# A graph network kernel: VectorE's order fixed around the attention scores, PSUM pools kept open, the last two tiles of a half taken together, additions on GpSimd

## The chip, the cores and the metric

The kernel runs on one core of one Trainium2 chip. The metric is the device time of one execution in microseconds. The kernel before takes 974.88 us (median of three runs, 974.85 to 976.33). Its profiled execution took 973.86 us, with a span of 972.1 us from the first to the last instruction that the profile counts.

## The reference

There are 625 nodes with 1024 features, 20000 edges sorted by destination, and 8 edge types. Two graph layers run one after the other, each with a residual and a layernorm.

```python
h = x @ W                                   # layer 0: attention
al, ar = h @ a_l, h @ a_r
e = exp(-leaky_relu(al[src] + ar[dst], 0.1))
h_prime = segment_sum(e[:, None] * h[dst], src) / (segment_sum(e, src)[:, None] + EPS)
x = layernorm(x + elu(h_prime))

u = x @ root + bias                         # layer 1: relational, gated
for r in range(8):
    mean = segment_sum(x[src] * (type == r), dst) / maximum(count, 1)
    u = u + mean @ weight[r]
z = concatenate([u, x], axis=1) @ w_gate + b_gate
x = layernorm(x + tanh(u) * z + x * (1 - z))
```

## The kernel before

The nodes lie in five tiles of 125 rows (`ST = 5`). The 1024 columns are worked on in two halves of 512, so that one product fills one PSUM bank.

**Counts.** Instead of gathering rows, the kernel builds dense counts: how many edges of each type run between each pair of nodes. One-hot matrices are made on VectorE (L808), multiplied on TensorE (L832), and copied by ScalarE into `cj` (L837), one `cj` for each tile j of destinations. Beside this TensorE computes `h` (L782), and VectorE takes the two row sums `al` and `ar` (L793). A list of due steps in the loop over `NGS` blocks says after which block row sums, spreading and counts are issued.

**Scores.** `all_types(j)` adds the eight types of `cj` in three VectorE additions, c4, c2 and c1 (L845, L847, L849). `scores_of(j)` then takes, for tile j, the sum of `ar` and `al` (L865), two operations for the edge mask and the leaky relu (L868, L869), an exponential on ScalarE (L870), a product with the counts (L871), and a row sum (L872). A small value `turn` (L874), made from the row sum of tile j and read by tile j + 1, makes the tiles go one after the other. `turn_scores(j)` transposes the scores on TensorE (L883) and ScalarE copies them to `attT` (L885). `gather_h(t, j)` multiplies them with `h` (L684). Tiles 0 to 2 (`EARLY = 3`) gather while the scores are made, tiles 3 and 4 afterwards. `sums` in the text below means L865.

**Dense products.** Each fp32 product is done in three passes with fp32r parts. `prepare(count)` splits a chunk of 128 rows of a weight into three pieces: g and e on ScalarE (L998, L999), m and the final e on VectorE (L1000, L1001). There are buffers for ten such units (`UNITS = 10`), and a half needs eight (`KC`). The nodes' rows are transposed and split likewise into h, l and d (`turned_pieces`, `pieces_of`, L1009 to L1011). `dense` takes a half: for each tile eight pairs of products into one bank (L1025, L1026), and eight into a second (L1029). In tile 0 the three are taken chunk by chunk; in the others the second bank comes after the first. Two units of the next half are prepared after tile 1 and six after the last tile.

**Order of the stages.** Scores and gathering; `attend(t)`, which makes the elu, the residual and the first layernorm of tile t (L1068 to L1078, with two small GpSimd operations for the deviation, L980 and L981); root in two halves; eight relations in two halves each, with the product by counts (`pu`, L1195); the gate's four halves wgx0, wgx1, wgu0, wgu1, during which `turn_u(t)` transposes and splits u (L1223); `mix` and the last layernorm. `ins` adds incoming counts (L1134, L1136), whose transposes (L1140) give the divisors.

**What sets the order.** Loads and stores all go through SP's queue. Within each engine the tile framework's scheduler fixes the order of instructions when the kernel is built: it takes what its own model of time calls ready first, and program order between equals. A tile pool that is closed and followed by another in the same place makes the new pool's first users wait for the last readers of the old one. Before, the PSUM pools of 6 and 2 banks are closed ahead of the first score transposes and a pool of 8 is opened.

## Time and profile before

| What | us |
|---|---|
| Median of three runs (lowest, highest) | 974.88 (974.85, 976.33) |
| Profiled execution | 973.86 |
| Its span | 972.1 |
| TensorE busy | 945.3 (97%) |
| VectorE busy | 597.2 (61%) |
| ScalarE busy | 391.4 (40%) |
| GpSimd busy | 39.5 (4%) |
| First score transposes begin | 111.51 |
| Last gathers end | 166.99 |
| First product of root begins | 167.62 |
| Gate halves begin | 844.72 |
| Last product ends | 960.4 |

The profile has one row for each instruction: start, duration, engine, line of the kernel, operation, output and input. In brackets stands how long the engine was idle before it and what ended the wait. TensorE is called PE there, its weight loads PEld, VectorE DVE, ScalarE ACT, GpSimd POOL, SyncE SP. One fp32 matmul shows as two records where the two operands are fp32. Rows that follow each other closely are merged ("x12"). A busy table gives each engine's busy time within chosen stretches, and the clock that TensorE was granted, 1.00 being full speed.

### The profile page before, as it was taken

The numbers are of one execution on the slowest core, as the hardware profiler recorded it, in microseconds if no ns is written. First come the engines' busy times: TensorE is split into PE (matmuls) and PEld (weight loads), VectorE is DVE, ScalarE is ACT, GpSimd is POOL, SyncE is SP. The second block draws the span as 40 slices with busy tenths as digits, with TensorE's granted clock in tenths as the row PEclk, the third lists the DMA queues.
The fourth block names the chain that finished last, engine by engine and source line by source line (L and its number), as shares of the span: only waits on it lengthen the run. The fifth ranks groups of instructions, "written<-read, shape, count | busy, mean of one in ns | idle before, by whom it ended". The sixth has DMA issues, their size and how long they took to land.

```text
span 972.1 us, 10853 instructions
## 1 busy us (share of the span) xinstructions
PE 945.3 (97%) x4075; PEld 730.5 (75%) x4075; DVE 597.2 (61%) x960; ACT 391.4 (40%) x714; POOL 39.5 (4%) x69
## 2 busy tenths in 40 slices
PE   7999699999999999999999999999999999999995
PEld 3555445878888888888888888888888888888874
DVE  1998978976626546356265364562653644639995
ACT  1333837244434515515434345244342551433422
POOL 3000001000000000000000000000000000002123
PEclk9999999999999999999999999999999999999998
DMA  8134862442103113021122120320320211432213
GB/s 298 44 78 102 198 197 75 141 155 87 65 22 121 45 42 108 21 80 66 55 87 63 59 87 23 99 76 11 121 66 22 87 37 50 139 112 74 87 39 112
DMA packets 61631, 83.89 MB, mean 86 GB/s; under 512 B 29323, under 2 KB 29735, under 8 KB 61572
## 3 DMA queue, kind: packets, MB, share of 16 engines
q1 hardware_dynamic: 61364, 82.93, 27.6%
q8 instruction: 34, 0.56, 0.2%
q14 instruction: 25, 0.20, 0.1%
q0 software_dynamic: 208, 0.19, 0.1%
HBM read 71.36 MB, written 11.75 MB: 86 GB/s over the span
## 4 chain that ended last, share of the span: by engine, by line
PE 92%; DVE 5%; ACT 1%; DMA 1%; SPq 0%; issue 0%; POOL 0%; POOLq 0%; DVEq 0%; ACTq 0%
PE pu L1195 19%; PE p_w L1026 15%; PE p_w L1025 15%; PE p_w L1029 15%; PE ph L782 7%; PE phh L684 3%; PE p_root L1029 2%; PE p_root L1025 2%; PE p_wgx L1029 2%; PE p_wgx L1026 2%; PE p_wgx L1025 2%; PE p_root L1026 2%; PE pc L832 2%; PE p_wgu L1029 1%; PE p_wgu L1026 1%; PE p_wgu L1025 1%
## 5 line engine op out<-in xcount | busy, mean ns | idle before, releaser
L1026 PE MATMUL p_w<-m_w,x_l 128*128 128x512 f32 x640 | 249.1, 389 | 0.0
L1025 PE MATMUL p_w<-g_w,x_h 128*128 128x512 f32 x640 | 249.0, 389 | 0.0
L1195 PE MATMUL pu<-y,cf 125*128 125x512 f32 x800 | 184.4, 389 | 0.0
L1177 DVE SCALAR_TENSOR_TENSOR v<-p_w,v 125x512 f32<-125x512 f32 x80 | 55.2, 690 | 201.7 <-PE p_w L1029 153.0
L1029 PE MATMUL p_w<-e_w,x_d 128*128 128x512 f32 x640 | 176.4, 389 | 0.0
L1195 PEld LDWEIGHTS pu<-y,cf 125*128 125x128 f32 x800 | 150.2, 188 | 31.6
L1029 PEld LDWEIGHTS p_w<-e_w,x_d 128*128 128x128 f32 x640 | 120.1, 188 | 25.5 <-DVE e_w L1001 0.3
L1025 PEld LDWEIGHTS p_w<-g_w,x_h 128*128 128x128 f32 x640 | 120.2, 188 | 25.1
L1026 PEld LDWEIGHTS p_w<-m_w,x_l 128*128 128x128 f32 x640 | 120.1, 188 | 25.1 <-DVE m_w L1000 0.2
L1176 ACT ACTIVATE v<-p_w 125x512 f32<-125x512 f32 x80 | 47.6, 595 | 214.0 <-PE p_w L1026 214.0
L1000 DVE SCALAR_TENSOR_TENSOR m_w<-raw_w,e_w 128x512 fp32r<-128x512 f32 x128 | 84.9, 684 | 36.3 <-ACT e_w L999 36.3
L1180 DVE TENSOR_TENSOR y<-v,y 125x512 fp32r<-125x512 f32 x80 | 55.3, 691 | 50.8 <-ACT y L1179 50.8
L998 ACT ACTIVATE g_w<-raw_w 128x512 fp32r<-128x512 f32 x128 | 73.2, 621 | 29.8 <-PE p_w L1025 20.7
L1001 DVE TENSOR_TENSOR e_w<-g_w,m_w 128x512 fp32r<-128x512 f32 x128 | 84.9, 684 | 0.5
L1179 ACT CAST y<-v 125x512 fp32r<-125x512 f32 x80 | 49.2, 615 | 75.1 <-DVE v L1177 75.1
L782 PE MATMUL ph<-w,xT 128*125 128x512 f32 x160 | 77.6, 612 | 0.3 <-ACT xT L714 0.3
L999 ACT ACTIVATE e_w<-raw_w 128x512 fp32r<-128x512 f32 x128 | 73.2, 623 | 0.0
L1199 DVE SCALAR_TENSOR_TENSOR L_gnn_bias_dram_u<-pu,inv,L_gnn_bias_dram_u 125x512 f32<-125x512 f32 x80 | 55.5, 743 | 0.5
L1161 ACT CAST cf<-cs 128x640 fp32r<-128x640 f16 x40 | 25.9, 724 | 54.8 <-PE pu L1195 46.2
L1242 POOL TENSOR_TENSOR L_gnn_bias_dram_u<-L_gnn_bias_dram_u,xr 125x512 f32<-125x512 f32 x10 | 17.4, 1743 | 744.2 <-ACT L_gnn_bias_dram_u L1227 712.0
L684 PE MATMUL phh<-h_sb,attT 125*125 125x512 f32 x100 | 45.9, 614 | 0.4 <-ACT attT L885 0.4
L782 PEld LDWEIGHTS ph<-w,xT 128*125 128x125 f32 x160 | 27.9, 192 | 24.1 <-issue 22.2
(159 smaller groups left out, 972.0 us busy)
## 6 DMA issues: line engine op xcount, KB each, us to landing
raw_w<-in_L_gnn_weight_dram SPq DMA_DIRECT2D x64, 512.0 KB
cd<-cj SPq DMA_DIRECT2D x40, 160.0 KB
cs<-cd SPq DMA_DIRECT2D x8, 800.0 KB
x<-in_x_dram SPq DMA_DIRECT2D x8, 512.0 KB
w<-in_L_gnn_W_dram SPq DMA_DIRECT2D x8, 512.0 KB
raw_root<-in_L_gnn_root_dram SPq DMA_DIRECT2D x8, 512.0 KB
raw_wgx<-in_L_gnn_w_gate_dram SPq DMA_DIRECT2D x8, 512.0 KB
raw_wgu<-in_L_gnn_w_gate_dram SPq DMA_DIRECT2D x8, 512.0 KB
```

What stands on the lines that cost most here:

```text
L684: nc.tensor.matmul(banks_h[t, half][:n, :], attT[:nj, j, tile_cols(t)], h_sb[:nj, j, half * HALF:(half + 1) * HALF], start=(j == 0), stop= ...
L782: nc.tensor.matmul(p[:n, :], xT[:, k, :n], w0_sb[k][:, half * HALF:(half + 1) * HALF], start=k == 0, stop=k == KC - 1)
L998: nc.scalar.activation(g, w, AF.Copy, scale=DOWN)
L999: nc.scalar.activation(e, w, AF.Copy, scale=UP12 * DOWN)
L1000: nc.vector.scalar_tensor_tensor(m, w, UP12, e.bitcast(F32), op0=OP.mult, op1=OP.subtract)
L1001: nc.vector.tensor_tensor(e, g.bitcast(F32), m.bitcast(F32), op=OP.subtract)
L1025: nc.tensor.matmul(p1, h[:, k, :], g, start=k == 0, stop=False, skip_group_check=True)
L1026: nc.tensor.matmul(p1, l[:, k, :], m, start=False, stop=k == KC - 1, skip_group_check=True)
L1029: nc.tensor.matmul(p2, d[:, k, :], e, start=k == 0, stop=k == KC - 1, skip_group_check=True)
L1180: nc.vector.tensor_tensor(lo[:n], v[:n], hi[:n].bitcast(F32), op=OP.subtract)
L1195: nc.tensor.matmul(p, c[:m, t, j * 128:(j + 1) * 128], piece[:m], start=(t == 0 and i == 0), stop=(t == ST - 1 and i == 1), skip_group_che ...
L1199: nc.vector.scalar_tensor_tensor(at, p[:n], inv[:n, j, r:r + 1], at, op0=OP.mult, op1=OP.add)
```

## The change

1. **VectorE's order.** `in_turn` ties an instruction behind the one that was written before it on its engine. It is an edge for the order of issue only, without a wait of its own. The chain runs from the first sum of the scores to root's pieces: sum and two operations of tile 0, the first operation of tile 1, the product of tile 0, the second operation of tile 1; then in each step j the row sum of j, c4 of tile j + 3 (for j below 2), the product of j + 1, c2 and c1 of tile j + 3, and the two operations of j + 2. The value `turn` goes. The first scores' two copies to `attT` move from ScalarE to VectorE and stand in the chain. `prepare(KC, pinned=True)` puts the m of root's eight units behind all of it.
2. **GpSimd.** The sums of tiles 1 to 4 (L865), one addition of each half of the normalizing for tiles 1 to 4 (L1073), and the four additions of `ins` (L1134, L1136) move from VectorE to GpSimd.
3. **PSUM.** The pools of 6 and 2 banks stay open to the end. Until the gathering each bank names its pool; later ones are dealt out in turn, six from the first pool and two from the second.
4. **Two tiles together.** With `goes_on`, `dense` takes tiles 3 and 4 chunk by chunk side by side, all three products for both tiles. This holds for root0, root1, wgx0, wgx1 and wgu0. `turn_u` of tiles 3 and 4 moves from wgx1 into wgu0, behind its tiles 0 and 1.

```diff
-    begin = ExitStack()
-    ps = [begin.enter_context(tc.tile_pool(name="f_ps0", bufs=6, space=bass.MemoryType.PSUM))]
-    ps_h = begin.enter_context(tc.tile_pool(name="f_ps_h", bufs=2, space=bass.MemoryType.PSUM))
-
-    def bank(name):
-        return ps[0].tile([128, 512], F32, tag="bank", name=name)
+
+    ps = [ctx.enter_context(tc.tile_pool(name=f"f_ps{n}", bufs=n, space=bass.MemoryType.PSUM)) for n in (6, 2)]
+    turns = []
+
+    def bank(name, pool=None):
+
+        if pool is None:
+            pool = len(turns) % 8 // 6
+            turns.append(name)
+        return ps[pool].tile([128, 512], F32, tag="bank", name=name)
+
+    def in_turn(ins):
+
+        tc.keep_in_program_order(ins)
 
...
         for half in range(2):
             if j == 0:
-                banks_h[t, half] = bank(f"phh_{t}_{half}")
+                banks_h[t, half] = bank(f"phh_{t}_{half}", 1 if t == EARLY else 0)
...
             n = rows_of(t)
-            halves_h = [ps_h.tile([128, 512], F32, tag="ph", name=f"ph_{t}_{half}") for half in range(2)]
+            halves_h = [bank(f"ph_{t}_{half}", 1) for half in range(2)]
...
-        def all_types(j, cj):
+        def all_types(j, part, put=lambda ins: None):
 
             n = rows_of(j)
-            c4 = attp.tile([128, ST, 4, 128], F16, name="c4")
-            c4 = c4[:, :, :, :n]
-            nc.vector.tensor_tensor(c4, cj[:, :, 0:4, :n], cj[:, :, 4:8, :n], op=OP.add)
+            if part == 0:
+                c4 = attp.tile([128, ST, 4, 128], F16, name="c4")[:, :, :, :n]
+                fours.append(c4)
+                put(nc.vector.tensor_tensor(c4, cjs[j][:, :, 0:4, :n], cjs[j][:, :, 4:8, :n], op=OP.add))
+                return
+            c4 = fours.pop()
             c2 = c4[:, :, 0:2, :]
-            nc.vector.tensor_tensor(c2, c2, c4[:, :, 2:4, :], op=OP.add)
-            c1 = attp.tile([128, ST, 128], F16, name=f"c1_{j}")
-            nc.vector.tensor_tensor(c1[:, :, :n], c2[:, :, 0, :], c2[:, :, 1, :], op=OP.add)
-            ct.append(c1[:, :, :n])
+            c1 = attp.tile([128, ST, 128], F16, name=f"c1_{j}")[:, :, :n]
+            ct.append(c1)
+            put(nc.vector.tensor_tensor(c2, c2, c4[:, :, 2:4, :], op=OP.add))
+            put(nc.vector.tensor_tensor(c1, c2[:, :, 0, :], c2[:, :, 1, :], op=OP.add))
...
-
-        turn = attp.tile([128, ST], F32, name="turn")
-        nc.vector.memset(turn[:, :1], 1.0)
-
-        def scores_of(j):
+        def sums_of(j, eng):
 
             n = rows_of(j)
-            cols = slice(j * 128, j * 128 + n)
-            c1 = ct[j]
-            e = attp.tile([128, ST, 128], F32, name=f"e_{j}")
-            e = e[:, :, :n]
-            nc.vector.tensor_tensor(e, ar_b[:, cols].unsqueeze(1).to_broadcast([128, ST, n]),
-                                    al.unsqueeze(2).to_broadcast([128, ST, n]), op=OP.add)
-
-            nc.vector.scalar_tensor_tensor(e, c1, turn[:, j:j + 1], e, op0=OP.min, op1=OP.mult)
-            nc.vector.scalar_tensor_tensor(e, e, SLOPE, e, op0=OP.mult, op1=OP.max)
-            nc.scalar.activation(e, e, AF.Exp, scale=-1.0)
-            nc.vector.tensor_tensor(e, e, c1, op=OP.mult)
-            nc.vector.tensor_reduce(rsum[:, :, j], e, axis=AX.X, op=OP.add)
-            if j + 1 < ST:
-                nc.vector.tensor_scalar(turn[:, j + 1:j + 2], rsum[:, 0, j:j + 1], 0.0, 1.0, op0=OP.min, op1=OP.add)
-            return e
+            e = attp.tile([128, ST, 128], F32, name=f"e_{j}")[:, :, :n]
+            i = eng.tensor_tensor(e, ar_b[:, j * 128:j * 128 + n].unsqueeze(1).to_broadcast([128, ST, n]),
+                                  al.unsqueeze(2).to_broadcast([128, ST, n]), op=OP.add)
+            es.append(e)
+            return i
+
+        def scores_of(j, parts=(0, 1)):
+
+            if 0 in parts:
+
+                in_turn(nc.vector.scalar_tensor_tensor(es[j], ct[j], 1.0, es[j], op0=OP.min, op1=OP.mult))
+            if 1 in parts:
+                in_turn(nc.vector.scalar_tensor_tensor(es[j], es[j], SLOPE, es[j], op0=OP.mult, op1=OP.max))
+                nc.scalar.activation(es[j], es[j], AF.Exp, scale=-1.0)
+
+        def times_edges(j):
+            in_turn(nc.vector.tensor_tensor(es[j], es[j], ct[j], op=OP.mult))
+
+        def sum_scores(j):
+            in_turn(nc.vector.tensor_reduce(rsum[:, :, j], es[j], axis=AX.X, op=OP.add))
 
         def turn_scores(j, e):
             n = rows_of(j)
             for t0, t1 in ((0, 3), (3, ST)):
-                p = bank(f"patt_{j}_{t0}")
+                p = bank(f"patt_{j}_{t0}", 1)
                 for t in range(t0, t1):
                     m = rows_of(t)
                     nc.tensor.transpose(p[:n, (t - t0) * TN:(t - t0) * TN + m], e[:m, t, :], ident[:m, :m])
                 c0, c1 = t0 * TN, t1 * TN
-                nc.scalar.copy(attT[:n, j, c0:c1], p[:n, :c1 - c0])
+                if j:
+                    nc.scalar.copy(attT[:n, j, c0:c1], p[:n, :c1 - c0])
+                else:
+                    in_turn(nc.vector.tensor_copy(attT[:n, j, c0:c1], p[:n, :c1 - c0]))
...
         def counted(j):
-            all_types(j, cjs[j])
+            if j < ST - 2:
+                all_types(j, 0)
+                all_types(j, 1)
             store_counts(j, cjs[j])
+
+        def first_scores(_):
+            spread_ar()
+            in_turn(sums_of(0, nc.vector))
+            for j in range(1, ST):
+                sums_of(j, nc.gpsimd)
+            scores_of(0)
+            scores_of(1, parts=(0,))
+            times_edges(0)
+            scores_of(1, parts=(1,))
...
                     if steps == n_steps:
-                        due.append((i + 6, lambda _: spread_ar(), None))
-                        due.extend((max(i + 6 + 4 * j, (j + 1) * NG + LAG), lambda _: es.append(scores_of(len(es))), None)
-                                   for j in range(AHEAD))
+                        due.append((i + 6, first_scores, None))
...
-        begin.close()
-        ps[0] = ctx.enter_context(tc.tile_pool(name="f_ps", bufs=8, space=bass.MemoryType.PSUM))
         for _ in range(4):
             fetch()
         turn_scores(0, es[0])
         for j in range(ST):
             gather_h(0, j)
-            if len(es) < ST:
-                es.append(scores_of(len(es)))
+
+            sum_scores(j)
             if j + 1 < ST:
+                later_types = j + 3 if j < 2 else None
+                if later_types:
+                    all_types(later_types, 0, in_turn)
+                times_edges(j + 1)
+                if later_types:
+                    all_types(later_types, 1, in_turn)
+                if j + 2 < ST:
+                    scores_of(j + 2)
                 turn_scores(j + 1, es[j + 1])
             for t in range(1, EARLY):
                 gather_h(t, j)
...
-    def prepare(count):
...
-            nc.vector.scalar_tensor_tensor(m, w, UP12, e.bitcast(F32), op0=OP.mult, op1=OP.subtract)
+            rest = nc.vector.scalar_tensor_tensor(m, w, UP12, e.bitcast(F32), op0=OP.mult, op1=OP.subtract)
+            if pinned:
+                in_turn(rest)
             nc.vector.tensor_tensor(e, g.bitcast(F32), m.bitcast(F32), op=OP.subtract)
             ready.append((g, m, e))
             if i == 1:
...
+    def dense_tiles(ts, chunks, name, by_chunk):
+
+        sums = {t: (bank(f"p1_{name}_{t}"), bank(f"p2_{name}_{t}")) for t in ts}
+
+        def first(t, k, g, m):
+            h, l, _ = x1[t]
+            nc.tensor.matmul(sums[t][0], h[:, k, :], g, start=k == 0, stop=False, skip_group_check=True)
+            nc.tensor.matmul(sums[t][0], l[:, k, :], m, start=False, stop=k == KC - 1, skip_group_check=True)
+
+        def second(t, k, e):
+            nc.tensor.matmul(sums[t][1], x1[t][2][:, k, :], e, start=k == 0, stop=k == KC - 1, skip_group_check=True)
 
         for k, (g, m, e) in enumerate(chunks):
-            first(k, g, m)
-            if t == 0:
-                second(k, e)
-        if t:
+            for t in ts:
+                first(t, k, g, m)
+                if by_chunk:
+                    second(t, k, e)
+        if not by_chunk:
             for k, (g, m, e) in enumerate(chunks):
-                second(k, e)
-        return p1, p2
-
-    def dense(name, put, after=None):
+                for t in ts:
+                    second(t, k, e)
+        return sums
+
+    def dense(name, put, after=None, goes_on=False):
 
         chunks = [ready.pop(0) for _ in range(KC)]
-        for t in range(ST):
-            n = rows_of(t)
-            p1, p2 = dense_tile(t, chunks, f"{name}_{t}")
-            put(t, p1[:n, :], p2[:n, :])
-            if t == 1:
-                prepare(UNITS - KC)
-            if after:
-                after(t)
+
+
+        steps = [(t,) for t in range(ST - 2)] + ([(ST - 2, ST - 1)] if goes_on else [(ST - 2,), (ST - 1,)])
+        for ts in steps:
+            for t, (p1, p2) in dense_tiles(ts, chunks, name, ts[0] == 0 or len(ts) > 1).items():
+                n = rows_of(t)
+                put(t, p1[:n, :], p2[:n, :])
+                if t == 1:
+                    prepare(UNITS - KC)
+                if after:
+                    after(t)
         prepare(2 * KC - UNITS)
...
-            nc.vector.tensor_add(v, q[:n], v)
+            (nc.gpsimd if t else nc.vector).tensor_tensor(v, q[:n], v, op=OP.add)
...
-    prepare(KC)
+    prepare(KC, pinned=True)
...
-    dense("root0", add_to(u, 0), after=later_x1)
+    dense("root0", add_to(u, 0), after=later_x1, goes_on=True)
...
-    nc.vector.tensor_tensor(ins, ins16[:, 0, :], ins16[:, 1, :], op=OP.add)
+    nc.gpsimd.tensor_tensor(ins, ins16[:, 0, :], ins16[:, 1, :], op=OP.add)
     for t in range(2, ST):
-        nc.vector.tensor_tensor(ins, ins16[:, t, :], ins, op=OP.add)
+        nc.gpsimd.tensor_tensor(ins, ins16[:, t, :], ins, op=OP.add)
...
-    dense("root1", add_to(u, 1))
+    dense("root1", add_to(u, 1), goes_on=True)
...
-    dense("wgx0", add_to(z, 0))
-    dense("wgx1", add_to(z, 1), after=turn_u)
-    dense("wgu0", mix(0))
+    dense("wgx0", add_to(z, 0), goes_on=True)
+    dense("wgx1", add_to(z, 1), after=lambda t: t < ST - 2 and turn_u(t), goes_on=True)
+    dense("wgu0", mix(0), after=lambda t: t < 2 and turn_u(t + ST - 2), goes_on=True)
```

More of the change, by code (lines that the diff above doesn't have):

```diff
@@ L455 @@
 LAG = 4
-AHEAD = 1
 EARLY = 3
@@ L665, in load_x, with transposed @@
         return xt
-    def transposed(src_t, n, name, put):
+    def transposed(src_t, n, name, put, pool=None):
         for g in range(2):
-            p = bank(f"{name}_{g}")
+            p = bank(f"{name}_{g}", pool)
             for j in range(4):
@@ L713, in x_turned @@
             xT = xin.tile([128, KC, 128], F32, tag="xT", name=f"xT_{t}")
-            transposed(xt, n, f"px_{t}", lambda ks, p: nc.scalar.copy(xT[:, ks, :n], p))
+            transposed(xt, n, f"px_{t}", lambda ks, p: nc.scalar.copy(xT[:, ks, :n], p), 0)
             if t + 2 < ST:
@@ L735, in gather_edges @@
         def gather_edges():
-            p = bank("p_count")
+            p = bank("p_count", 0)
             for m in range(per // BLOCK):
@@ L752, in place_edges @@
         def place_edges():
-            pe = bank("p_edges")[:, :4 * NGS]
+            pe = bank("p_edges", 0)[:, :4 * NGS]
             for b in range(2):
@@ L768, in place_edges @@
                                            op0=OP.mult, op1=OP.add)
-        ct = []
+        ct, fours = [], []
         s_hots = [hot.tile([128, 2, BG, 2, 128], F16, name=f"s_hot_{i}", bufs=1) for i in range(HOTS)]
@@ L828, in counts_of @@
             s_hot, m_hot, _ = built[i]
-            p = bank(f"pc_{i}")
+            p = bank(f"pc_{i}", 0)
             at = 0
@@ L916, in spread_ar @@
             for t0, t1 in ((0, 3), (3, ST)):
-                p = bank(f"p_ar_{t0}")
+                p = bank(f"p_ar_{t0}", 0)
                 for t in range(t0, t1):
@@ L988, in fast, with prepare @@
     xp = ctx.enter_context(tc.tile_pool(name="f_x1", bufs=1, side="right"))
-    def prepare(count):
+    def prepare(count, pinned=False):
         for _ in range(count):
@@ L1017, in turned_pieces @@
         transposed(src_t, 128, f"p{name}_{t}", lambda ks, p: pieces_of(h, l, d, ks, p))
-    def dense_tile(t, chunks, name):
-        h, l, d = x1[t]
-        p1, p2 = bank(f"p1_{name}"), bank(f"p2_{name}")
-        def first(k, g, m):
-            nc.tensor.matmul(p1, h[:, k, :], g, start=k == 0, stop=False, skip_group_check=True)
-            nc.tensor.matmul(p1, l[:, k, :], m, start=False, stop=k == KC - 1, skip_group_check=True)
-        def second(k, e):
-            nc.tensor.matmul(p2, d[:, k, :], e, start=k == 0, stop=k == KC - 1, skip_group_check=True)
-        for k, (g, m, e) in enumerate(chunks):
-            first(k, g, m)
-            if t == 0:
-                second(k, e)
-        if t:
+    def dense_tiles(ts, chunks, name, by_chunk):
[6 more added lines that the diff above has]
+            nc.tensor.matmul(sums[t][1], x1[t][2][:, k, :], e, start=k == 0, stop=k == KC - 1, skip_group_check=True)
+        for k, (g, m, e) in enumerate(chunks):
+            for t in ts:
[3 more added lines that the diff above has]
+        if not by_chunk:
```

## The prediction

> **What bounds the kernel now.** I read the page's engine shares first, then the busy table by stage, TensorE's own timeline where the table shows it idle, VectorE's timeline over the same stretch, and last the places where GpSimd and VectorE meet.
>
> ```profile
> PE 945.3 (97%) x4075; PEld 730.5 (75%) x4075; DVE 597.2 (61%) x960; ACT 391.4 (40%) x714; POOL 39.5 (4%) x69
> ```
>
> TensorE sets the time: it is idle for 27 us of 972.1. The table finds these in three places: 6 us at the start and 11.6 us behind the last matmul, which the change leaves alone, and the scores, from 109 to 140 us:
>
> ```profile
> 109.00:112.00 3.00, 0.49 (x5) 0.52 (x5) 3.00 (x5) 2.94 (x7) 0.00 (x0) 1.00 0.98 201
> 114.70:119.50 4.80, 0.00 (x0) 0.00 (x0) 4.80 (x9) 4.77 (x10) 0.86 (x1) 0.82 0.73 150
> 119.50:122.00 2.50, 2.44 (x7) 1.88 (x8) 2.50 (x7) 1.71 (x4) 0.09 (x1) 0.50 0.90 235
> 122.00:124.00 2.00, 2.00 (x3) 0.67 (x2) 2.00 (x4) 0.63 (x1) 0.00 (x0) 0.50 0.78 222
> 124.00:126.00 2.00, 2.00 (x5) 0.90 (x4) 2.00 (x4) 1.78 (x4) 0.00 (x0) 0.85 0.73 269
> ```
>
> The columns are TensorE, its weight loads, VectorE, ScalarE, GpSimd, the granted clock and DMA. VectorE is full while TensorE stands still, and behind the long stop the clock is granted at half (0.50). TensorE's timeline there:
>
> ```profile
> 104.09 4.92 PE L832 MATMUL pc<-m_hot,s_hot 128*128 128x240 f16 x42
> 111.51 0.78 PE L883 MATMUL patt<-ident,e 125*125 125x125 f32 x5 [2.50 <-DVE e L871]
> 112.69 1.98 PE L684 MATMUL phh<-h_sb,attT 125*125 125x512 f32 x4 [0.40 <-ACT attT L885]
> 119.56 1.41 PE L883 MATMUL patt<-ident,e 125*125 125x125 f32 x5 [4.89 <-DVE e L871]
> 120.76 7.22 PE L684 MATMUL phh<-h_sb,attT 125*125 125x512 f32 x12
> 128.36 5.32 PE L684 MATMUL phh<-h_sb,attT 125*125 125x512 f32 x12
> ```
>
> The idle times are 2.50 + 0.40 + 4.89 and 0.21 later, 8.0 us; the half clock costs 0.5 x 4.44 + 0.15 x 2.0 = 2.5 us (7.22 against 5.32 for the same twelve records). **10.5 us** are there to be had. The clock's mean of 0.82 over 4.8 us says that it fell some 3.1 us into the stop; the 2.50 did not bring it down. What kept the second scores:
>
> ```profile
> 111.28 1.47 DVE L845 TENSOR_TENSOR c<-cj 128x2500 f16<-128x2500 f16 x1
> 117.49 1.29 DVE L1000 SCALAR_TENSOR_TENSOR m_root<-raw_root,e_root 128x512 fp32r<-128x512 f32 x2
> 118.70 0.81 DVE L871 TENSOR_TENSOR e<-e,c 128x625 f32<-128x625 f32 x1
> ```
>
> The edge sums of tile 4, two sums of later scores and root's pieces stand between the first scores (done 111.36) and the second (119.51): 8.15 us.
>
> **The change, part by part.** *VectorE's order.* It takes c4 of tiles 3 and 4 (1.38), four sums (0.72 each) and m_root out of the way. ar_b is there at 105.0. Without any contention e_0 is: sum 0.72, two operations 0.78 + 0.73, exponential 0.73 and hand-over, product 0.72: 108.9. TensorE has counts until 109.01, so the first gap would be nothing; keeping the PSUM pools open, which lets the transposes go before ScalarE's last copy (110.65), is worth something only if e_0 is early. But the order fixed also puts the second scores' first operation, which needs GpSimd's sum e_1, ahead of e_0's product: product, copies and all that follow queue behind that wait.
>
> *Sums on GpSimd.* Its addition of 512 columns takes 1.29 us undisturbed; 625 columns are an estimated 1.58. And it disturbs VectorE:
>
> ```profile
> 892.72 1.29 POOL L1242 TENSOR_TENSOR L_gnn_bias_dram_u<-L_gnn_bias_dram_u,xr 125x512 f32<-125x512 f32 x1 [5.04 <-ACT L_gnn_bias_dram_u L1227]
> 892.87 2.29 DVE L1011 SCALAR_TENSOR_TENSOR u_d<-u_l,u_h 128x512 fp32r<-128x512 f32 x2
> ```
>
> Two such operations take 1.29 elsewhere, so 1.00 is lost here. Over the ten GpSimd additions of the trace VectorE's neighbours lose 0 to 1.0, 0.56 in the mean. The Trainium skill speaks against this edit, in "SBUF — State Buffer", section "Who interferes with whom": a VectorE instruction with two SBUF inputs and a GpSimd instruction that reads SBUF use the same port, and whichever starts second is blocked until the other has finished. All of e_0's operations have two SBUF inputs. By the rule, taking turns, four additions stand in the chain: 105.0 + 3.75 + 4 x 1.58 = 115.1. By the rows: 105.0 + 2.23, e_1's addition 1.58, 0.78, 0.72 and one block of 0.56 are 110.9. I take 110.9, since back-to-back VectorE work kept GpSimd waiting in the trace (one addition took 2.70 with no loss to VectorE). First gap: 1.9, with ends 0 and 6.1.
>
> *The first copies on VectorE.* By the PSUM rows (512 columns 0.68), 375 columns cost an estimated 0.5, then 0.35; the gap behind the transposes stays 0.5.
>
> *The second scores.* Behind the product: 0.73, copies 0.95 with their wait, row sum 0.72, c4 1.38, product 0.72, and two blocks of 0.56: 116.5. TensorE, after transposes (0.78), copy (0.5) and all six gathers of step 0 (5.32), is there at 117.5: no gap. If the second transposes again stand behind two gathers only, it is there at 114.0: gap 2.5. I take 1.2. From then each step costs TensorE 0.71 + 5.32 = 6.03 and VectorE at most 5.5, so no gap grows. No stop reaches 3.1 us, so no half clock. Idle 1.9 + 0.5 + 1.2 = 3.6; the stage gains 10.5 - 3.6 = **6.9**, ends 1.4 (first gap 6.1, then 0.5, and the clock's 2.5 paid again) and 10.0.
>
> *Root's pieces behind the scores.* VectorE ends the scores at 116.5 + 13.3 = 129.8 and the reciprocals at 130.4; 16 operations of 0.60 end at 140.0. The cover is the 5.5 us in which it waits before its first normalizing operation (146.61, which comes 6.9 earlier, 139.7): cost nothing now, but that cover is used up. The five loads of weights (SP, 118.8 to 138.1) wait for these pieces and shift by some 8 us; the loads of x stand among them in SP's queue and are wanted at 139.7, the second half of root at 192: hidden.
>
> *Additions in the normalizing.* Eight of 0.68 leave VectorE (5.4); by the rows 8 x 0.56 = 4.5 come back, by the rule 8 x 1.3 = 10.4. GpSimd's rstd operations (0.55 + 0.57) queue behind the next tile's additions; x of tiles 1 to 3 is ready 7 us ahead of its transposes, so this is covered. The four additions of ins on GpSimd (an estimated 1.6 each for 3.2 on VectorE) delay the p_ins transposes in root1, 0 to 3 us. Together I take 0.5.
>
> *Two tiles together.* Units come free during the last two tiles, not in the last pass. The first two tiles of a half need 2 x 5.44 = 10.88; they take 11.26 (transposes off), 11.24 and 12.60 in the three gate halves, and up to 0.5 extra in root1: 2.5 to 3.0 lost. The longest stop:
>
> ```profile
> 942.12 2.11 PE L1029 MATMUL p_wgu<-e_wgu,u_d 128*128 128x512 f32 x8 [0.61 <-DVE e_wgu L1001]
> ```
>
> The table's row for the stretch before it:
>
> ```profile
> 898.00:929.00 31.00, 31.00 (x142) 25.31 (x141) 30.05 (x46) 14.35 (x28) 5.60 (x4) 1.00 0.24 76
> ```
>
> VectorE is busy 30.05 of these 31 us, and the change takes nothing off it there. Turning u's tiles 3 and 4 (8 transposes of 0.87 in all, four VectorE operations of 0.64, two tanh each) moves behind wgu0's tiles 0 and 1, where mixing already takes five operations of 0.69 per tile of 5.44: 3.4 + 2.6 is more than a tile, so these pieces come late by 1 to 2 us, with one tile of 5.44 in between as cover. Earlier units therefore help only partly: I take 1.0, ends -1.0 (no cover: the pair waits for u's pieces) and 2.5 (nothing lost any more). In root0 the pair brings tile 4's pieces forward:
>
> ```profile
> 185.86 1.03 PE L673 MATMUL px<-ident,x 128*128 128x128 f32 x8
> 187.13 1.29 DVE L1010 TENSOR_TENSOR x_l<-px,x_h 128x512 fp32r<-128x512 f32 x2
> 188.34 1.29 DVE L1011 SCALAR_TENSOR_TENSOR x_d<-x_l,x_h 128x512 fp32r<-128x512 f32 x2
> ```
>
> Before, d was wanted at 195.8; now 0.7 us into the pair, 187.3 on this scale, and its first half is there at 188.9: a wait of 1.6, or nothing if TensorE's queue has tile 3 in front. I take 0.7.
>
> **Sum:** 6.9 + 1.0 - 0.5 - 0.7 = 6.7. The span of 972.1 becomes 965.4; with the 1.8 around it (973.86 - 972.1) the profiled run becomes 967.2. The runs' median stands 1.0 above the profiled one: 974.88 - 6.7 = **968.2**.
>
> **Rivals.** *Likeliest, 0.56:* as summed; its own range is 964.5 to 971.5 (first gap 0.5 to 3.5, second 0 to 2.5).
> *All gaps close, 0.09:* VectorE's chain runs ahead of GpSimd and the gathers cover the second scores: 10.0 + 1.0 - 0.5, about 964 to 963. For it: GpSimd's 2.70; against it: the queue behind e_1.
> *GpSimd in turns, 0.18:* the four sums take turns with e_0's chain. The stage gains 1.4, the halves pay the pair: 973 to 976, mostly no change. For it: 1.00 lost on single additions.
> *Slower, 0.17:* VectorE becomes the bound at root0's pair. If each of the eight additions blocks it by b, it is 8b - 5.4 late and TensorE waits 1.6 + 8b - 5.4 at the pair. This outweighs 6.9 + 1.0 - 0.5 when b is above 1.4. At 1.6 the wait is 9.0, the half clock adds 2.5, and the time is 974.88 + 1.6 + 2.5 = 979. For it: VectorE is busy 38.9 of the 43.4 us from 146.6 to 190; against it: no row shows b above 1.0.
>
> **Chances.** About 0.2% (2 us) is what a measurement of this kernel can tell from no change. Faster: 0.56 + 0.09 + a third of GpSimd in turns = 0.71; same: 0.11, most of the rest of it; slower: 0.18. The range, leaving out little above and below, is 963.5 to 977.
>
> **What would show it.** The transposes of e_0 start near 111.0, those of e_1 near 117; no row at clock 0.50 after 112; the last transposes end near 136 with all earlier gathers done; m_root begins at 130. GpSimd's sums show 1.6 to 2.1, VectorE's products beside them up to 1.0 more than 0.80. In the pair, a wait on x_d. In the last half no stop on e_wgu. Wrong makes it a stop over 3 us before the first transposes, a pair wait over 3 us, or p_ins late.

## The result and the profile after

The changed kernel takes **979.25 us** (median of five runs, 978.52 to 980.88), against 975.29 for the kernel before in the same comparison: a ratio of 1.0043 with an interval of 1.0028 to 1.0058. It is slower by 0.43%, where 0.7% faster was forecast, and it lies outside the range given. The profiled execution took 978.52 us, with a span of 976.7.

From the page of the changed kernel:

```profile
PE 947.7 (97%) x4075; PEld 734.0 (75%) x4075; DVE 604.0 (62%) x941; ACT 393.5 (40%) x712; POOL 61.4 (6%) x85
```

VectorE gave sixteen additions away (with the five small instructions of `turn` gone and two copies come in, 960 instructions became 941), and yet its busy time rose from 597.2 to 604.0. What is left on it got longer. The stages, by the starts of their first products and the end of the last (960.55 before, 964.15 after):

| Stage | before, us | after, us | difference |
|---|---|---|---|
| up to root's first product | 167.6 | 163.2 | -4.4 |
| root, two halves | 59.4 | 70.1 | +10.6 |
| relations, eight times two halves | 617.7 | 617.4 | -0.3 |
| gate, four halves | 115.8 | 113.5 | -2.3 |
| behind the last product | 11.6 | 12.6 | +1.0 |

These add up to the +4.6 between the spans. The scores and the gate gained; root lost more than both. The view of what TensorE waited for, in the changed kernel (us in total, times, longest):

```profile
PE patt L894 <- DVE e L883: 3.6, 1, 3.6
PE p_root L1058 <- DVE x_l L1042: 3.1, 1, 3.1
PE p_all L1183 <- DVE in_r L1181: 2.5, 1, 2.5
```

Before, the two long waits were 4.9 and 2.5, both at `patt`. Now there are three, all on VectorE, two of them in root, where there was none. The busy table of the changed kernel around them (columns as in the prediction):

```profile
109.00:112.60 3.60, 0.03 (x1) 0.00 (x0) 3.60 (x4) 2.55 (x5) 2.96 (x2) 1.00 0.80 164
114.00:116.00 2.00, 2.00 (x3) 0.94 (x4) 2.00 (x3) 2.00 (x6) 0.00 (x0) 0.60 0.00 0
116.00:118.00 2.00, 2.00 (x4) 0.75 (x3) 1.97 (x4) 2.00 (x5) 0.00 (x0) 0.54 1.01 210
...
170.00:173.10 3.10, 0.00 (x1) 0.00 (x0) 2.11 (x5) 0.55 (x2) 1.33 (x3) 0.89 0.88 285
173.10:175.00 1.90, 1.86 (x4) 1.49 (x5) 1.90 (x4) 0.00 (x0) 0.73 (x1) 0.50 1.00 351
...
177.00:179.00 2.00, 2.00 (x6) 1.52 (x6) 1.56 (x4) 0.00 (x0) 0.79 (x2) 0.50 0.90 235
...
200.00:202.50 2.50, 0.05 (x1) 0.00 (x0) 2.50 (x5) 0.58 (x2) 0.00 (x0) 1.00 0.87 318
204.00:206.00 2.00, 2.00 (x6) 1.52 (x6) 2.00 (x4) 0.00 (x0) 0.00 (x0) 0.50 0.52 174
```

In this trace each stop is followed by some microseconds at half clock, which cost half their length: about 1.7 us behind the first, 2.9 behind the second, 1.7 behind the third. TensorE's timeline behind the first stop:

```profile
112.68 0.81 PE L894 MATMUL patt<-ident,e 125*125 125x125 f32 x5 [3.65 <-DVE e L883]
114.00 5.37 PE L691 MATMUL phh<-h_sb,attT 125*125 125x512 f32 x8 [0.51 <-DVE attT L899]
119.21 0.71 PE L894 MATMUL patt<-ident,e 125*125 125x125 f32 x5
```

The second scores no longer make TensorE wait (119.21 has no bracket). The first do, and the reason is beside them, in the timeline of VectorE and GpSimd:

```profile
104.79 0.81 DVE L868 TENSOR_TENSOR e<-ar_b,al 128x625 f32<-128x625 f32 x1 [0.89 <-ACT ar_b L935]
105.64 1.72 DVE L877 SCALAR_TENSOR_TENSOR e<-c,e 128x625 f32<-128x625 f16 x1
107.39 1.72 DVE L879 SCALAR_TENSOR_TENSOR e<-e 128x625 f32<-128x625 f32 x1
109.04 1.83 DVE L877 SCALAR_TENSOR_TENSOR e<-c,e 128x625 f32<-128x625 f16 x1
110.79 1.83 DVE L883 TENSOR_TENSOR e<-e,c 128x625 f32<-128x625 f32 x1
...
104.84 7.12 POOL L868 TENSOR_TENSOR e<-ar_b,al 128x625 f32<-128x625 f32 x4 [5.53 <-ACT ar_b L935]
```

Four additions on GpSimd, 1.78 each, and exactly four operations of VectorE that take 1.72 to 1.83 where they take 0.81 alone: each pays 0.9 to 1.0. (The second row at L877 is the first operation of tile 1, which the fixed order puts ahead of e_0's product.) The same in the normalizing and ahead of root1:

```profile
164.41 1.28 POOL L1109 TENSOR_TENSOR x<-q,x 125x512 f32<-125x512 f32 x1
164.48 1.76 DVE L1114 TENSOR_SCALAR x<-x,mv,rstd 125x1024 f32<-125x1024 f32 x1 [0.77 <-POOL rstd L1011]
167.37 1.40 DVE L1030 SCALAR_TENSOR_TENSOR m_root<-raw_root,e_root 128x512 fp32r<-128x512 f32 x1
172.40 1.28 DVE L1042 TENSOR_TENSOR x_l<-px,x_h 128x512 fp32r<-128x512 f32 x2
173.14 0.79 PE L1058 MATMUL p_root<-m_root,x_l 128*128 128x512 f32 x1 [3.13 <-DVE x_l L1042]
...
192.16 2.94 DVE L1030 SCALAR_TENSOR_TENSOR m_root<-raw_root,e_root 128x512 fp32r<-128x512 f32 x2 [0.72 <-ACT e_root L1029]
192.79 5.41 POOL L1172 TENSOR_TENSOR ins<-ins,ins 8x640 f32<-8x640 f16 x3
195.01 3.74 DVE L1033 TENSOR_TENSOR e_root<-g_root,m_root 128x512 fp32r<-128x512 f32 x2
...
201.69 0.80 DVE L1181 TENSOR_REDUCE in_r<-ins 8x1 f32<-8x640 f32 x1
202.54 0.18 PE L1183 MATMUL p_all<-ones,in_r 8*1 8x1 f32 x2 [2.49 <-DVE in_r L1181]
```

The scaling of x takes 1.76 where it takes 0.81, and two pairs of pieces take 2.94 and 3.74 where such a pair takes 1.29. At 167.37 there is something else: a piece of root1's first units, which before was done by 138.7, stands in the middle of the normalizing, ahead of tile 1's x_l (172.40). And in_r, which p_all waits for, starts at 201.69, although GpSimd is done with ins at 198.20: root1's pieces stand before it.

### The profile page after: what moved, and what is told of

It is laid out like the page before. It is cut to its first block, busy times and chain, and to the rows that moved or that the text cites. A ratio compares the mean times of both kernels' runs of the same rounds, so it can differ in the third digit from the quotient of the medians.

```text
span 976.7 us, 10888 instructions
## 1 busy us (share of the span) xinstructions
PE 947.7 (97%) x4075; PEld 734.0 (75%) x4075; DVE 604.0 (62%) x941; ACT 393.5 (40%) x712; POOL 61.4 (6%) x85
## 4 chain that ended last, share of the span: by engine, by line
PE 89%; DVE 6%; ACT 1%; issue 1%; POOL 1%; DMA 1%; SPq 0%; POOLq 0%; DVEq 0%; ACTq 0%
PE pu L1231 19%; PE p_w L1057 15%; PE p_w L1058 15%; PE p_w L1061 15%; PE ph L789 7%; PE phh L691 2%; PE p_wgx L1057 2%; PE p_wgx L1058 2%; PE p_wgx L1061 2%; PE p_root L1057 2%; PE pc L839 2%; PE p_root L1058 2%; PE p_root L1061 1%; PE p_wgu L1057 1%; PE p_wgu L1058 1%; PE p_wgu L1061 1%
## 5 line engine op out<-in xcount | busy, mean ns | idle before, releaser
L1278 POOL TENSOR_TENSOR L_gnn_bias_dram_u<-L_gnn_bias_dram_u,xr 125x512 f32<-125x512 f32 x10 | 14.0, 1405 | 739.0 <-ACT L_gnn_bias_dram_u L1263 718.5
```

## The experiments

**First theory:** the additions on GpSimd take VectorE's turns, and that is the loss. **Rival:** the fixed order of VectorE, or the two tiles together, makes the stops. Four kernels undo the GpSimd part, group by group and whole.

*The sums of the scores back on VectorE.*

```diff
-            for j in range(1, ST):
-                sums_of(j, nc.gpsimd)
             scores_of(0)
+            in_turn(sums_of(1, nc.vector))
...
+                    in_turn(sums_of(j + 2, nc.vector))
                     scores_of(j + 2)
```

> After the change, with the four sums of the scores (e_1 to e_4) back on VectorE, each just ahead of the scores that use it; all else as after. Theory (additions on GpSimd take VectorE's turns): the four VectorE operations of 1.72 to 1.83 us beside the sums fall back to about 0.80, e_0 is ready near 109.5 instead of 112.6, the stop of 3.65 us ahead of the first transposes of scores shrinks below 1 and the half clock from 114 to 118 (about 1.8 us) goes: 4 to 5.5 us faster than the changed kernel, 973.5 to 975. Rival (the fixed order of VectorE, not GpSimd, sets the first stop): the stop stays above 3 us and the time is within 1 us of the changed kernel, 978 to 980.

Measured: 975.62 us, ratio to the kernel before 1.0004 (0.9995 to 1.0012), so 3.6 us under the changed kernel. Its timeline:

```profile
107.01 0.81 DVE L877 SCALAR_TENSOR_TENSOR e<-c,e 128x625 f32<-128x625 f16 x1
111.01 0.81 PE L894 MATMUL patt<-ident,e 125*125 125x125 f32 x5 [0.61 <-DVE e L883]
...
200.15 0.18 PE L1183 MATMUL p_all<-ones,in_r 8*1 8x1 f32 x2 [2.48 <-DVE in_r L1181]
```

The operations are back at 0.81, the stop is 0.61 and its half clock is gone. That the additions lengthen these operations and make the first stop is shown; the gain is a little below what was expected. A stop of 2.2 at tile 1 and the one of 2.5 at p_all stay.

*The normalizing additions back on VectorE.*

```diff
-            (nc.gpsimd if t else nc.vector).tensor_tensor(v, q[:n], v, op=OP.add)
+            nc.vector.tensor_tensor(v, q[:n], v, op=OP.add)
```

> After the change, with the normalizing additions of tiles 1 to 4 back on VectorE; all else as after. Theory (turns): the eight beside-operations lose about 0.7 us each and x_l of tile 1 is ready 3 us or more earlier, so the stop of 3.13 us at root0's tile 1 and its half clock (about 2.8 us) go: 4.5 to 6.5 us faster, 972.5 to 974.5. Rival (units 9 and 10 of root's pieces, which now land inside the normalizing, make x_l late): the stop only shrinks by about 1 us, the half clock stays: 0 to 2 us faster, 977 to 979.

Measured: 977.70 us, 1.0026 (1.0016 to 1.0035), only 1.6 us under the changed kernel. The stop of 3.1 at tile 1 is gone with its half clock, more than the rival allowed, though the held pieces are still there. But TensorE then stands 2.1 us ahead of tile 4's transposes, 0.9 at tile 4's x_l and 3.3 ahead of root1. The rival's number was right, its reason was not: relief on VectorE at one place comes back as stops at the next.

*The additions of ins back on VectorE.*

```diff
-    nc.gpsimd.tensor_tensor(ins, ins16[:, 0, :], ins16[:, 1, :], op=OP.add)
+    nc.vector.tensor_tensor(ins, ins16[:, 0, :], ins16[:, 1, :], op=OP.add)
     for t in range(2, ST):
-        nc.gpsimd.tensor_tensor(ins, ins16[:, t, :], ins, op=OP.add)
+        nc.vector.tensor_tensor(ins, ins16[:, t, :], ins, op=OP.add)
```

> After the change, with the four additions of the in-degrees back on VectorE; all else as after. Theory (turns): the operations of VectorE beside them fall from 2.94 and 3.74 us a pair to 1.29, the stop of 2.49 us ahead of root1 and its half clock to 206 (about 1.8 us) go: 3.5 to 4.5 us faster, 974.5 to 975.5. Rival (the two tiles taken together leave no cover at root0's end, so in_r is late whoever adds): the stop stays at 2 us or more, at most 1 us faster, 978 to 979.

Measured: 976.92 us, 1.0020 (1.0011 to 1.0028): 2.3 us, less than expected. The stop of 2.5 at p_all goes; one of 0.8 at p_ins and one of 0.3 behind it are left.

*All three groups back on VectorE* (the three diffs together).

> After the change, with all three groups of additions back on VectorE, so that only the fixed order, the open PSUM pools and the two tiles together remain. Theory (GpSimd's additions are the whole loss): the three gains add up to 12 to 15 us, 964 to 967, faster than the kernel before by 0.8 to 1.1%. Rival (the fixed order delays root's stage by itself): a stop of over 2 us stays at root0's tile 1 and the time is 970 to 975.

Measured: 972.09 us, 0.9972 (0.9960 to 0.9983). GpSimd's part costs **7.2 us** in the changed kernel, close to the sum of the three (7.5). But 964 to 967 was expected. Root0 begins at 159.0 here, 8.6 us earlier than before, and still root takes 66.5 us for the 59.4 of before: stops of 1.2, 0.8 and 1.4 between 177 and 182, and half clock behind them. The first theory explains most of the loss, not all of it.

**Second theory:** from the scores to root0's last tile VectorE is the bound, and what TensorE gains in the scores only lets it run into VectorE. **Rival:** the two tiles taken together ask too early.

*Without GpSimd's additions, root1's first two units after root0's tile 3.*

```diff
-                if t == 1:
+                if t == (ST - 2 if name == "root0" else 1):
                     prepare(UNITS - KC)
```

> The kernel without GpSimd's additions (972.1), with the pieces of root1's first two units made after root0's tile 3 instead of after its tile 1; all else as there. Theory (VectorE's own queue from the end of the scores to tile 4's x sets root0's end): four operations of 0.60 us, 2.4 us, leave that queue, x of tile 4 is scaled near 178.7 instead of 181.1, the stops of 1.2, 0.8 and 1.4 us at tile 3 shrink to about 1 in sum and the half clock behind them (1.6 us) goes: 968 to 969.8. Rival (the two tiles taken together ask for tile 4's pieces too early, whatever VectorE's load): the stops stay and the time is 971 to 973.

Measured: 970.38 us, 0.9951 (0.9935 to 0.9968). x of tile 4 is scaled at 178.67, as worked out, instead of 181.07; but the units then go ahead of tile 4's x_l, which makes a stop of 2.1 behind one of 1.6. The time is between the two expectations and, with 1.7 us under the kernel that it varies, not outside what the two intervals leave.

*Without GpSimd's additions, root0's tiles 3 and 4 one after the other.*

```diff
-    dense("root0", add_to(u, 0), after=later_x1, goes_on=True)
+    dense("root0", add_to(u, 0), after=later_x1)
```

> The kernel without GpSimd's additions (972.1), with root0's last two tiles taken one after the other again; the other halves still take them together. Theory (VectorE's queue): tile 4's transposes stand ahead of most of tile 3's matrix multiplications in either form and wait for the same x at 181: 971 to 973. Rival (the two tiles together are what asks too early): the three stops of root0 and its half clock go, 3.5 to 5 us: 967 to 968.6.

Measured: 975.13 us, 1.0000 (0.9990 to 1.0009): neither; it is 3.0 us worse than with the pair. Its timeline and a row of its busy table:

```profile
181.57 0.81 DVE L1114 TENSOR_SCALAR x<-x,mv,rstd 125x1024 f32<-125x1024 f32 x1 [0.45 <-POOL rstd L1011]
182.44 1.97 PE L680 MATMUL px<-ident,x 128*128 128x128 f32 x8 [2.39 <-DVE x L1114]
...
182.40:188.00 5.60, 5.56 (x18) 4.75 (x19) 4.37 (x7) 1.19 (x2) 0.00 (x0) 0.51 0.33 101
```

TensorE waits for tile 4's x as the theory said, and works 5.6 us at half clock. So the pair does not make this stop. What makes it 3.0 us slower is in good part the clock: in the two traces TensorE's stops in root add up to 4.4 us here and 4.0 with the pair, while the half clock costs about 4.2 and 1.7. Here a second stretch of it follows, from 204 to 208, behind a stop of 0.8 ahead of root1; with the pair a stop of 0.7 there has none. The rest was not traced.

*The kernel before, with the two tiles together and the moved turns of u alone.*

```diff
-    dense("root0", add_to(u, 0), after=later_x1)
+    dense("root0", add_to(u, 0), after=later_x1, goes_on=True)
...
-    dense("root1", add_to(u, 1))
+    dense("root1", add_to(u, 1), goes_on=True)
...
-    dense("wgx0", add_to(z, 0))
-    dense("wgx1", add_to(z, 1), after=turn_u)
-    dense("wgu0", mix(0))
+    dense("wgx0", add_to(z, 0), goes_on=True)
+    dense("wgx1", add_to(z, 1), after=lambda t: t < ST - 2 and turn_u(t), goes_on=True)
+    dense("wgu0", mix(0), after=lambda t: t < 2 and turn_u(t + ST - 2), goes_on=True)
```

> The kernel before with the last two tiles of a half taken together, and the two turns of u moved, alone. Theory: the gate stage gains 2.3 us as in the changed kernel, and root0's pair waits 1 to 2 us for tile 4's pieces, which were ready at 188.4 where the pair would start at 186.7: 973 to 974.8. Rival (the pair in root0 costs several us by itself): 975.5 or more.

Measured: 983.69 us, 1.0089 (1.0072 to 1.0106). The expectation was wrong by 9 us, and in the direction of the rival. The wait for tile 4's pieces is hardly there. In its place (timeline, then busy table):

```profile
196.44 0.80 DVE L1138 TENSOR_TENSOR ins<-ins 8x640 f32<-8x640 f16 x1
204.05 0.81 DVE L1140 TENSOR_TENSOR ins<-ins,ins 8x640 f32<-8x640 f16 x1
204.95 0.34 PE L1144 MATMUL p_ins<-ident,ins 8*125 8x8 f32 x1 [6.26 <-issue]
205.46 0.80 DVE L1149 TENSOR_REDUCE in_r<-ins 8x1 f32<-8x640 f32 x1
...
198.50:205.00 6.50, 0.24 (x2) 0.08 (x1) 6.50 (x11) 0.92 (x2) 0.00 (x0) 0.69 0.27 81
205.00:210.00 5.00, 4.36 (x12) 2.54 (x12) 2.31 (x8) 0.00 (x0) 0.00 (x0) 0.50 0.77 263
```

The profile puts the wait down to no instruction ("issue"), but p_ins begins 0.09 us behind the last addition of ins (204.86). The first addition and in_r in the kernel before:

```profile
191.20 0.80 DVE L1134 TENSOR_TENSOR ins<-ins 8x640 f32<-8x640 f16 x1
...
195.06 0.81 DVE L1145 TENSOR_REDUCE in_r<-ins 8x1 f32<-8x640 f32 x1
```

With tiles 3 and 4 singly, VectorE adds tile 3's sums to u, does the additions of ins while TensorE works on tile 4, and turns to root1's pieces last. With the pair, no sums come before the pair ends; root1's pieces fill VectorE's queue first and ins comes behind and between them: its first addition starts 5 us later, in_r 10 us later. TensorE's queue has p_ins and p_all ahead of root1, so it stands 6.3 us and then works at half clock until 214.5. The order is read from the rows; why the scheduler chose it was not looked into.

*Without GpSimd's additions, root's pieces not held behind the scores.*

```diff
-    prepare(KC, pinned=True)
+    prepare(KC)
```

> The kernel without GpSimd's additions (972.1), with root's pieces no longer held behind the scores in VectorE's order, as before the change. Theory (VectorE's work up to tile 4's x is the same in any order, and it has no idle time to give): the pieces go between the scores again, root0 starts 3 to 5 us later and loses its stops: 970 to 973.5. Rival (holding the pieces behind the scores is what makes x late): the scores keep their gain and root0 its pace, 966.5 to 968.5.

Measured: 970.77 us, 0.9961 (0.9945 to 0.9977), as the theory had it; the 1.3 us under the kernel with held pieces are within the intervals. Root0 begins at 162.0, three us later (one of them because the scores themselves begin later in this trace); one stop of 0.4 is left in it, and 0.8 at p_ins behind it.

**What is left to tell apart:** which parts are good, and whether the root0 pair's harm is the order of ins.

*The order of the scores and the open PSUM pools alone:* the kernel just shown, with all halves singly and `turn_u` back in wgx1.

```diff
-    dense("root0", add_to(u, 0), after=later_x1, goes_on=True)
+    dense("root0", add_to(u, 0), after=later_x1)
...
-    dense("root1", add_to(u, 1), goes_on=True)
+    dense("root1", add_to(u, 1))
...
-    dense("wgx0", add_to(z, 0), goes_on=True)
-    dense("wgx1", add_to(z, 1), after=lambda t: t < ST - 2 and turn_u(t), goes_on=True)
-    dense("wgu0", mix(0), after=lambda t: t < 2 and turn_u(t + ST - 2), goes_on=True)
+    dense("wgx0", add_to(z, 0))
+    dense("wgx1", add_to(z, 1), after=turn_u)
+    dense("wgu0", mix(0))
```

> The kernel before with the change's order of the scores and the open PSUM pools alone: no additions on GpSimd, root's pieces not held behind the scores, no two tiles together. Theory (VectorE's queue up to tile 4's x caps what the scores give): root0 starts near 162 instead of 167.6, about 2 of the 5.6 us come back as stops in root0, and the gate keeps its own pace: 970.5 to 972.5. Rival (the score stage's gain passes whole): 968 to 970.

Measured: **968.50 us**, 0.9931 (0.9913 to 0.9949). The rival holds: root0 begins at 162.3 and takes no stop, root lasts 59.4 us, and the score stage's gain passes whole. The second theory, that VectorE caps what the scores can give, was too strong. The order, the open pools, the end of `turn` and the copies on VectorE were not tried one by one, so the gain belongs to them together.

*The kernel before with pairs in every half but root0's* (the diff of the pairs alone, without its first two lines).

> The kernel before with the last two tiles together in every half but root0's. Theory (in root0 the pair lets root1's pieces go ahead of the in-degrees' additions in VectorE's order, and TensorE then stands 6 us and runs 4 us at half clock): all of that goes and the gate's 2.3 us stay, 972 to 973.5, that is 10 to 12 us less than with root0's pair. Rival (the loss of the pairs alone comes from any of the pairs, by their PSUM banks): 978 to 984.

Measured: 973.66 us, 0.9985 (0.9978 to 0.9992), 10 us under the kernel with root0's pair, as expected, though 0.2 above the range. In its trace the gate takes 113.5 us, for 115.8 before, and root 59.4, for 70.2 with root0's pair.

*Order of the scores, and pairs in every half but root0's.*

```diff
-    dense("root0", add_to(u, 0), after=later_x1, goes_on=True)
+    dense("root0", add_to(u, 0), after=later_x1)
```

> The kernel of the run without GpSimd's additions and with unheld pieces (970.8), with root0's last two tiles one after the other. Theory: the additions of the in-degrees go ahead of root1's pieces again, so the stop of 0.8 us at p_ins and the half clock of 1.7 us from 202 to 206 go: 968 to 970. Rival (as with the held pieces, taking root0's tiles singly costs 3 us): 973 to 974.5.

Measured: **966.67 us**, 0.9908 (0.9892 to 0.9925), below the expected range, and the fastest of all: 0.9% faster than the kernel before. Busy table and timeline, with the table's rows of the kernel before behind them:

```profile
104.00:140.00 36.00, 33.27 (x142) 18.19 (x140) 34.97 (x55) 25.07 (x53) 0.95 (x1) 1.00 0.73 204
140.00:160.00 20.00, 20.00 (x54) 9.10 (x53) 18.43 (x34) 15.38 (x26) 2.16 (x4) 1.00 0.32 106
...
177.89 0.81 DVE L1114 TENSOR_SCALAR x<-x,mv,rstd 125x1024 f32<-125x1024 f32 x1 [1.00 <-POOL rstd L1011]
```

```profile
104.00:140.00 36.00, 28.00 (x108) 15.14 (x108) 35.54 (x55) 22.97 (x48) 0.95 (x1) 0.91 0.78 209
140.00:160.00 20.00, 20.00 (x57) 9.33 (x56) 12.71 (x26) 12.27 (x22) 2.16 (x4) 1.00 0.15 50
```

VectorE idled 7.3 us between 140 and 160 before; now 1.6. TensorE is busy 33.27 us instead of 28.00 in the scores, at full clock. All ten units' pieces are done by 144.3, in the holes of the scores' chain and just behind it; x of tile 4 is scaled at 177.9. In the kernel that differs from this one only by the held pieces, root0 begins 3.5 us earlier, two of the units fall into the normalizing, and x of tile 4 is scaled at 181.6. (Times of day in two traces compare only roughly: the first sum of the scores starts at 107.14 here and at 105.64 there. Counted from it, root0 begins 2.0 earlier there and x of tile 4 is scaled 5.2 later.)

*The changed kernel with root0's tiles singly.*

```diff
-    dense("root0", add_to(u, 0), after=later_x1, goes_on=True)
+    dense("root0", add_to(u, 0), after=later_x1)
```

> The changed kernel with root0's last two tiles one after the other; GpSimd's additions and the held pieces stay. Theory: tile 3's and tile 4's sums are added to u in turn, in_r is ready before root0 ends, so the stop of 2.5 us ahead of root1 and its half clock (1.8 us) go, while the stop at tile 1 stays: 975 to 976.5. Rival (the stop ahead of root1 is GpSimd's contention alone): it stays, 978 to 980.

Measured: 975.44 us, 1.0002 (0.9994 to 1.0011), as expected: root0's pair costs **3.8 us** in the changed kernel. The stop of 2.5 at p_all is gone, that of 3.1 at tile 1 stays.

*The fastest kernel with the three groups on GpSimd again* (the changed kernel, pieces not held and root0's tiles singly).

```diff
-    prepare(KC, pinned=True)
+    prepare(KC)
...
-    dense("root0", add_to(u, 0), after=later_x1, goes_on=True)
+    dense("root0", add_to(u, 0), after=later_x1)
```

> The fastest kernel so far (966.7: the change without GpSimd's additions, with unheld pieces and root0's tiles singly) with the three groups of additions on GpSimd again. Theory (the additions cost by themselves, since VectorE is busy without a break from the scores to root0's end and shares its turns): the first stop of 3.6 us with its half clock and a stop in root0 return, 972.5 to 975. Rival (they cost only because the held pieces and the pair had filled VectorE's queue): 968 to 971.

Measured: 969.87 us, 0.9939 (0.9920 to 0.9957): 3.2 us for the additions, in the rival's range. The stop of 3.6 before the first scores returns as the theory had it; in root0 only 0.5 is left.

*The changed kernel with the pieces not held.*

```diff
-    prepare(KC, pinned=True)
+    prepare(KC)
```

> The changed kernel with root's pieces no longer held behind the scores; the additions on GpSimd and root0's pair stay. Theory (the three GpSimd groups make the stop at tile 1, holding adds little while the pair is there, 1.3 us as without GpSimd): 976.5 to 979. Rival (the held pieces make that stop): it goes with its half clock, 972 to 975.

Measured: 975.39 us, 0.9999 (0.9990 to 1.0007), near the rival. What TensorE waited for:

```profile
PE p_all L1183 <- DVE in_r L1181: 2.5, 1, 2.5
...
PE p_root L1058 <- DVE x_l L1042: 0.5, 1, 0.5
```

The stop at tile 1 is gone (the 0.5 comes at tile 2, 177.81), and the held pieces cost **3.9 us** in the changed kernel. It was gone as well when only the normalizing additions went back to VectorE: this stop needs both, and undoing either removes it.

The three suspects in all their combinations, with the order of the scores and the other pairs in place throughout (us; ratio to the kernel before):

| Pieces held | Root0's pair | GpSimd's additions off | GpSimd's additions on |
|---|---|---|---|
| no | no | 966.67 (0.9908) | 969.87 (0.9939) |
| no | yes | 970.77 (0.9961) | 975.39 (0.9999) |
| yes | no | 975.13 (1.0000) | 975.44 (1.0002) |
| yes | yes | 972.09 (0.9972) | 979.25 (1.0043) |

They don't add. GpSimd costs 0.3 to 7.2, held pieces 1.3 to 8.5, and the pair 3.8 to 5.5, but in one row it gains 3.0. Each makes VectorE late somewhere between 104 and 206 us. Some stops need two of them: that at tile 1 the held pieces and the normalizing additions; that at p_all comes with the pair and is 2.5 with the additions of ins on GpSimd, 0.8 and 0.3 without. And whether the half clock follows makes steps of some two microseconds. As one ladder: 975.2 before, -6.7 for the order of the scores with the open pools, -1.8 for the pairs outside root0, +4.1 for root0's pair, +1.3 for holding the pieces, +7.2 for GpSimd, 979.3. Each step is uncertain by 1.5 to 2 us, so those of 1.3 and 1.8 alone are not clear of it; the pairs outside root0 alone, added to the kernel before, give 1.5 (0.8 to 2.1).

## Why the prediction was wrong

Three steps failed: the first gap of the scores (sums on GpSimd), root's pieces put at nothing, and root0's pair put at 0.7. Undone alone in the changed kernel they give 3.6, 3.9 and 3.8 us.

**The score stage's 6.9.** The kernel with the order alone gains 6.7 by the two medians, but it has neither the sums on GpSimd nor the held pieces from which 6.9 was summed, so the agreement is partly luck. In the changed kernel root begins only 4.4 earlier. The failed step is *sums on GpSimd*: e_0 was put at 110.9 and its transposes start at 112.68; the first gap is 3.65 where 1.9 was taken; and "no stop reaches 3.1 us, so no half clock" fell with it (1.7 us). That threshold was read from one stop of one trace, and the last section shows that it does not hold. The prediction weighed the Trainium skill's rule ("SBUF — State Buffer", section "Who interferes with whom") against averaged rows, and chose the rows. The rule named the mechanism: the trace has one lengthened operation of VectorE for each addition. Its sum of 115.1 was too long, since a block cost 0.9 to 1.0, not the whole 1.58; with 0.95 the same sum is 105.0 + 3.75 + 4 x 0.95 = 112.6, and e_0 is done at 112.62. One block of 0.56 was counted where there were four of 0.95. The mean of 0.56 came mostly from single additions, for some of which VectorE lost nothing (in the one of 2.70 GpSimd itself took longer); four additions in a row beside a chain without gaps cost nearly the largest row, 1.00, each time.

**The other steps of the scores** held: 0.51 behind the first transposes for 0.5, no gap at the second scores where 1.2 was taken, the last transposes at 134.6 for 136.

**Root's pieces, "cost nothing now, but that cover is used up".** This step fails without GpSimd too (1.3 us with root0's pair, 8.5 without it). The cover was used up, and more was behind it: two units of root1, done by 138.7 before, were pushed into the normalizing, ahead of tile 1's x_l. The prediction did not ask which instructions stand next in VectorE's queue once the eight units end, at 144.5. Cost in the changed kernel: 3.9 us, where the normalizing additions on GpSimd are needed for the stop at tile 1 as well.

**Additions in the normalizing and ins, 0.5 together.** The block was mis-sized, and what the additions saved was nearly all paid back: the eight operations beside the normalizing additions lost 5.6 us, 0.7 each, against the 5.4 taken off VectorE. The additions of ins stretched two pairs of pieces by 1.65 and 2.45, and p_all came 2.5 late with 1.7 of half clock: the stop is inside the named "0 to 3" (p_ins itself was not late), the clock was not in it. Undone alone they give 1.6 and 2.3; all GpSimd parts together 7.2.

**Two tiles together, 1.0 less 0.7.** The gate's gain was under-sized, 1.0 for a measured 2.3, but right in sign and mechanism: no stop on e_wgu is left. For root0 the wrong instruction was looked at. The pair waits for no x_d; it takes 11.2 us for 10.9. The loss is at its end, where ins stands behind root1's pieces: 10 us when it is added to the kernel before with the other pairs (983.69 against 973.66), 3.8 in the changed kernel.

**The rivals.** "GpSimd in turns" (0.18) had the mechanism of the first stop, with 973 to 976. "Slower" (0.17) had the number, 979, and the right idea that VectorE becomes the bound in root, but its condition, a block above 1.4 per addition, was not met: no block in the scores or the normalizing exceeds 1.1. So its 979 is a coincidence. The loss needed neither the wait at the pair nor that size, since the held pieces and the order of ins had taken the slack.

## What to carry to other kernels

When a stage gets shorter, look up in the next stage how far the feeding engine is ahead, and follow its queue: the instruction that is pushed back can be the one that will be waited for. Moving operations to an engine that slows a busy one is to be costed by the largest loss in the rows, once for each of them that stands beside work without gaps, not by the mean of all rows. And a change that delays when results are released (two tiles at once) also changes what the scheduler puts ahead of the small work that the next stage needs.

## What the runs showed of the hardware

The half clock does not need one long stop, and the same stop does not always bring it. The kernel before and the one with all pairs but root0's have the same instructions up to root. Ahead of the first transposes TensorE stands 2.50 us in one trace and 2.51 in the other. Then come these rows of the busy table, the kernel before first, with clocks of 1.00 and 0.50:

```profile
112.00:116.00 4.00, 2.27 (x7) 0.77 (x5) 4.00 (x7) 4.00 (x10) 0.00 (x0) 1.00 1.04 215
```

```profile
112.00:116.00 4.00, 3.80 (x9) 1.90 (x8) 4.00 (x7) 3.64 (x9) 0.00 (x0) 0.50 1.03 212
```

At p_all the changed kernel stands 2.49 us, with one tiny transpose of 0.27 ahead of it, and the clock falls; the kernel with the sums back on VectorE stands 2.48 us there, and the clock stays at 1.00 until 208. The stop of 3.65 brought the clock down in all six traces that have it, but the half clock cost about 1.7 us in three of them and about 2.5 in the others. In the kernel with held pieces and single tiles, without GpSimd's additions, stops of 1.20 and 2.39 with two products between them were followed by a clock of 0.51. Without GpSimd's additions and with unheld pieces, root0's pair in place, only 0.78 and 0.33 of stop were seen around 199 us, and yet the clock was 0.50 from 202.4 to 205.7. No run tells why. So a stretch of half clock in one trace is in part chance, and only the medians over several runs carry a comparison.

An addition on GpSimd that took 1.28 us cost VectorE's neighbour 0.95, in a scaling with one tensor as input just as in operations with two.
